# Spreading the first convolutions of later batches over seven ticks less in a chain of long convolutions and a Haar layer

## The chip, the cores and the metric

The kernel runs on one core of one Trainium2 chip. The metric is the device time of one execution in microseconds (us), as the median of several runs. TensorE does the matmuls, VectorE and ScalarE read its results out of PSUM and do the element-wise work, SyncE and ScalarE issue the DMAs.

## The reference, cut to what matters

The input x has 4 batches of 64 channels of 256 x 256 float32 values. Four layers follow each other:

```python
x = conv(x, L0); x = conv(x, L1)      # long separable convolutions, zero padded, per channel, plus x * bias
f1 = haar2d(x)                        # all levels, along both axes
for i in range(2):
    f4 = einsum('bchw,oc->bohw', f1 * v[i], conv_w[i])      # mixes the channels
    acc += sign(f4) * relu(abs(f4) - tau[i])                # soft threshold
x = haar2d(acc, inverse=True) + x
x = conv(x, L3)
```

A convolution of one channel is two Toeplitz contractions, one along each axis. The Haar layer needs all 64 channels of a batch before it can mix them, and the last convolution needs the mixed coefficients of all rows.

## The kernel before

**Stages of one batch.** The function `convolutions` takes each channel through both first layers and the forward Haar transform, `mixing` takes 64 groups of coefficients through the channel mix and the threshold, and `inverse` takes each channel back through the inverse Haar transform and through the last convolution. Two thirds of the last convolutions of batches 0 to 2 are done in `inverse`; a third (`put_off`) are stored and done beside the mixing of batch 3 by `convolution`.

**Ticks.** No stage issues its work directly. Each puts its steps into a list of events through `at(tick, place, run, unit)`, and at the end the list is sorted by tick, then by place, and run in that order. So the tick of a step decides which other steps stand beside it in the program. The engines take their instructions in order; the framework adds the waits and may move independent instructions past each other on a queue.

**Steps of a channel in `convolutions`.** With its tick t: load at t; `first` of layer 0 at t+1 (contraction into the PSUM tile pa by lines 167 and 168, copied to a by ScalarE on line 176); `second` of layer 0 at t+2 (contraction into py, line 189 adds the bias term on VectorE into y); the same for layer 1 at t+3 and t+4, where `pairs` also makes the first Haar level along the row (lines 230 and 231 into the buffer sd) and stores the result in keep (line 232, by ScalarE's DMA queue). After every fourth channel, `levels` makes the other Haar levels of four channels in place in sd: three steps in three ticks, 14 VectorE operations (lines 240 and 241), each working on half the elements of the last. `down` then makes the Haar levels along the other axis by one matmul for each channel (pz, line 263), ScalarE copies it (line 267), and SyncE stores it in coef. The last `down` comes 11 ticks after the last channel's tick at most. sd has room for eight channels, so a group's levels and the next group's pairs don't share memory.

**Steps of a group in `mixing`.** mix (four px matmuls, line 308; scaling by VectorE on line 325 and by eight ScalarE operations on line 327), shrink (Abs and Sign on ScalarE, lines 333 and 334; a subtraction on line 335), signed (line 340), add (line 344, into the large buffer z), one tick apart. The next group starts one tick later.

**Steps of a channel in `inverse`.** fetch (load r; copy a column of z into zc on ScalarE, line 361; before channel 0, `butterfly` on z), rows (pw, lines 368 and 369; copy and subtraction into w, lines 371 and 372), cols (pu, line 381; t on line 385, u on lines 388 and 389), then the two contractions of the last convolution and the store of its result.

**What sets the ticks around the change.** Mixing of batch b takes the ticks from `start` on. The inverse begins at `end`, which is `start` + 67, and the next mixing begins at `end` + 64 or three ticks after the next batch's coefficients are ready, whichever is later. The convolutions of batch b+1 have to lie somewhere beside these. `spread(begin, end)` gives the 64 channels evenly spaced ticks from begin to just below end:

```python
def spread(begin, end, n=C):
    return [begin + i * (end - begin - 1) // (n - 1) for i in range(n)]
```

`ahead` is 64 for batch 1 and three ticks before `start` for batches 2 and 3.

Of the kernel before, what the change touches and what calls it, by code (L numbers as in the profile page):

```python
# [37 lines left out]
def conv_seq_kernel(ctx, tc, x, fz, fw, bias, decay, haar, haar_row, factors, vt, taut, wmix, out):  # L38
# [116 lines left out]
    def toeplitz(layer, c, name):  # L155

        t = tp.tile([P, 2, S], F32, name=name, tag="toep")
        nc.sync.dma_start(t, ap(pads[layer], c * 2 * ROW, [[1, P], [ROW, 2], [1, S]]))
        return t

    def bank(name):
        return psm.tile([P, 2, S], F32, name=name, tag="mm")
# [7 lines left out]
    def first(b, st, key, layer, new):  # L170
        def run(c):
            s = st[c]
            ps = bank(f"p{new}_{b}_{c}")
            contract(ps, s[key], s[layer][:, 0, :])
            a = io.tile([P, 2, S], F32, name=f"{new}_{b}_{c}", tag="mid")
            nc.scalar.copy(a, ps)  # L176
            s[new] = a

        return run

    def second(b, st, key, layer, res, new, tag, ahead=None):
        def run(c):
            s = st[c]
            if ahead is not None:
                s[ahead] = toeplitz(ahead, c, f"t{ahead}_{b}_{c}")
            ps = bank(f"p{new}_{b}_{c}")
            contract(ps, s[key], s[layer][:, 1, :])
            y = io.tile([P, 2, S], F32, name=f"{new}_{b}_{c}", tag=tag, bufs=BUFS[tag])
            nc.vector.scalar_tensor_tensor(y, s[res], bsb[:, layer, c : c + 1], ps, ALU.mult, ALU.add)  # L189
            s[new] = y  # L190

        return run
# [12 lines left out]
    def at(tick, place, run, unit):  # L205
        events.append((tick, place, len(events), run, unit))

    def stream(stages, ticks):

        for unit, tick in enumerate(ticks):  # L210
            for s, stage in enumerate(stages):
                if stage is not None:
                    at(tick + s, -s, stage, unit)

    def convolutions(b, ticks, in_parts=False):

        st = {}

        def load(c):
            xt = io.tile([P, 2, S], F32, name=f"x_{b}_{c}", tag="in", bufs=4)  # L220
            nc.sync.dma_start(xt, x[b, c].rearrange("(k p) w -> p k w", p=P))
            st[c] = {"x": xt, 0: toeplitz(0, c, f"t0_{b}_{c}")}

        last_second = second(b, st, "a1", 1, "y0", "y1", "res")

        def pairs(c):
            last_second(c)
            v = st.pop(c)["y1"].rearrange("p k (w e) -> p k w e", e=2)
            t = sd[:, c % 8]
            nc.vector.tensor_add(t[:, :, 0, :], v[:, :, :, 0], v[:, :, :, 1])  # L230
            nc.vector.tensor_sub(t[:, :, 1, :], v[:, :, :, 0], v[:, :, :, 1])  # L231
            nc.scalar.dma_start(keep[b][c], t)

        def levels(steps):
            def run(n):
                t = sd[:, n % 2 * 4 : n % 2 * 4 + 4]
                for step in steps:
                    v = t[:, :, :, 0, :].rearrange("p c k (w e) -> p (c k) w e", e=2 * step)
                    even, odd = v[:, :, :, 0], v[:, :, :, step]
                    nc.vector.tensor_sub(odd, even, odd)  # L240
                    nc.vector.scalar_tensor_tensor(even, even, 2.0, odd, ALU.mult, ALU.subtract)

            return run

        parts = {}

        def split(c):

            w = parts[c] = mx.tile([P, 2, 2, S], F32R, name=f"sp_{b}_{c}", tag="f4")
            t = sd[:, c % 8].rearrange("p k e w -> p k (e w)")  # L250
            nc.scalar.copy(w[:, 0], t)
            nc.vector.tensor_tensor(w[:, 1], t, w[:, 0].bitcast(F32), ALU.subtract)

        def down(c):
            ps = bank(f"pz_{b}_{c}")
            flat = "p k w -> p (k w)"
            if in_parts:
                for i in range(2):
                    nc.tensor.matmul(
                        ps.rearrange(flat), hbr, parts[c][:, i].rearrange(flat), start=(i == 0), stop=(i == 1)  # L260
                    )
            else:
                nc.tensor.matmul(
                    ps.rearrange(flat), hbt, sd[:, c % 8].rearrange("p k e w -> p (k e w)"), start=True, stop=True
                )
            t = io.tile([P, 2, S], F32, name=f"co_{b}_{c}", tag="co", bufs=BUFS["co"])
            nc.scalar.copy(t, ps)
            nc.sync.dma_start(coef[b][:, c].rearrange("k p w -> p k w"), t)

        stream(  # L270
            [load, first(b, st, "x", 0, "a0"), second(b, st, "a0", 0, "x", "y0", "y", ahead=1), first(b, st, "y0", 1, "a1"), pairs],
            ticks,
        )
        for n in range(C // 4):
            end = ticks[4 * n + 3] + 4
            for s, steps in enumerate([(1,), (2, 4), (8, 16, 32, 64)]):
                at(end + 1 + s, 1, levels(steps), n)
            for j in range(4):
                if in_parts:
                    at(end + 3 + j, 2, split, 4 * n + j)  # L280
                at(end + 4 + j, 2, down, 4 * n + j)
        return ticks[-1] + 11
# [128 lines left out]
    def convolution(which, ticks):  # L411

        for (b, c), tick in zip(which, ticks):
            st = {}

            def load(c, b=b, st=st):
                u = io.tile([P, 2, S], F32, name=f"v_{b}_{c}", tag="in", bufs=4)
                nc.sync.dma_start(u, late[b, c])
                st[c] = {"u": u, 2: toeplitz(2, c, f"t2_{b}_{c}")}

            for s, stage in enumerate([load, *last(b, st)]):
                at(tick + s, -s, stage, c)


    def spread(begin, end, n=C):
        return [begin + i * (end - begin - 1) // (n - 1) for i in range(n)]
# [4 lines left out]
    ready = convolutions(0, range(C), in_parts=True)  # L431
    ahead = C
    start = ready + 3
    for b in range(B):
        mixing(b, start, 8 if b + 1 < B else 6)
        end = start + groups + 3
        if b + 1 < B:
            ready = convolutions(b + 1, spread(ahead, end + 2))
        else:
            convolution(  # L440
                [(i, c) for i in range(B - 1) for c in sorted(put_off)], spread(start - 2, end + 2, (B - 1) * len(put_off))
            )
        inverse(b, end, put_off if b + 1 < B else ())

        start = max(end + C, ready + 3)
        ahead = start - 3
# [112 lines left out]
```

## Time and profile before

The time is 3088.14 us as the median of three runs (3085.73 to 3089.94); the profiled execution spans 3090.0 us. The table cuts that execution at the first and the last px matmul of each mixing and at channel 20's row transform in the inverse. Busy times are in us.

| stretch | from, to (us) | length | PE | DVE | ACT | DMA share |
|---|---|---|---|---|---|---|
| mixing, batch 0 | 479.7 to 901.3 | 421.6 | 414.6 | 382.3 | 308.4 | 0.65 |
| mixing to inverse, batch 0 | 901.3 to 1005.8 | 104.5 | 98.1 | 75.2 | 57.7 | 0.71 |
| rest of the inverse, batch 0 | 1005.8 to 1142.4 | 136.6 | 136.6 | 110.2 | 86.8 | 0.78 |
| mixing, batch 1 | 1142.4 to 1601.4 | 459.0 | 452.6 | 403.5 | 317.1 | 0.67 |
| mixing to inverse, batch 1 | 1601.4 to 1712.1 | 110.7 | 106.1 | 78.7 | 60.4 | 0.71 |
| rest of the inverse, batch 1 | 1712.1 to 1848.6 | 136.5 | 136.5 | 110.1 | 86.7 | 0.78 |
| mixing, batch 2 | 1848.6 to 2309.4 | 460.8 | 454.1 | 403.4 | 317.0 | 0.67 |
| mixing to inverse, batch 2 | 2309.4 to 2419.7 | 110.3 | 104.8 | 78.4 | 60.2 | 0.73 |
| rest of the inverse, batch 2 | 2419.7 to 2552.3 | 132.6 | 132.6 | 109.4 | 86.2 | 0.79 |

PE is TensorE, DVE VectorE, ACT ScalarE. A row's idle TensorE time is its length less its PE time. A busy TensorE isn't TensorE at its peak, since a matmul's recorded end overlaps the next one's start; how far matmuls lie apart is read from their starts in the timeline.

### The profile page before, as it was taken

What the parts mean: (1) busy time and instruction counts of PE and PEld (TensorE: products, weight loads), DVE (VectorE), ACT (ScalarE), POOL (GpSimd) and SP (SyncE); (2) the same over time, 40 slices, a digit from 0 to 9 for tenths busy, and PEclk for the clock granted to TensorE, in tenths of its full rate; (3) what the DMA queues carried; (4) which work ended last, traced back from release to release, by engine and by line L of the source; (5) the groups of instructions that cost most, each with busy time, mean ns of one, the idle gap of its engine ahead of it and who ended that gap; (6) DMA issues with size and microseconds to landing.
All of it is one profiled execution on the core that took longest, in us unless ns stands there. A gap on an engine that the chain in (4) does not pass through costs nothing. (4 is left out here: it accounts for less than half of the span.)

```text
span 3090.0 us, 50474 instructions
## 1 busy us (share of the span) xinstructions
PE 3004.4 (97%) x16944; PEld 2615.3 (85%) x16944; DVE 2523.4 (82%) x4453; ACT 1926.9 (62%) x4054; POOL 0.2 (0%) x4
## 2 busy tenths in 40 slices
PE   5999999999999999999999999999999999999999
PEld 3999988888888888888887888888887888888998
DVE  6667677999987878888886879888886889998776
ACT  1333336777765656667665656666774667887554
POOL 0000000000000000000000000000000000000000
PEclk9999999999999999999999999999999999999999
DMA  4777877666667876666667776666667777877676
GB/s 118 217 230 230 234 227 211 196 193 197 195 193 228 238 223 196 195 207 199 194 205 216 236 229 196 199 195 204 198 195 218 235 238 228 236 233 212 210 211 188
DMA packets 555573, 649.26 MB, mean 210 GB/s; under 512 B 39761, under 2 KB 440500, under 8 KB 555188
## 3 DMA queue, kind: packets, MB, share of 16 engines
q1 hardware_dynamic: 439316, 493.18, 56.5%
q10 hardware_dynamic: 116000, 152.87, 13.7%
q8 instruction: 136, 2.23, 0.3%
q14 instruction: 121, 0.99, 0.1%
HBM read 426.40 MB, written 219.48 MB: 209 GB/s over the span
## 5 line engine op out<-in xcount | busy, mean ns | idle before, releaser
L167 PE MATMUL py<-t,a 128*128 128x256 f32 x3072 | 926.0, 383 | 27.9 <-ACT a L176 24.6
L176 ACT COPY a<-pa 128x512 f32<-128x512 f32 x768 | 458.7, 597 | 466.3 <-PE pa L168 330.7
L168 PEld LDWEIGHTS py<-t,a 128*128 128x128 f32 x3072 | 584.1, 190 | 79.4
L327 ACT ACTIVATE f<-px,vt 128x64 f32<-128x64 f32 x1920 | 422.0, 329 | 352.7 <-DVE f L325 348.3
L167 PEld LDWEIGHTS py<-t,a 128*128 128x128 f32 x3072 | 488.4, 191 | 126.1 <-issue 63.2
L168 PE MATMUL py<-t,a 128*128 128x128 f32 x3072 | 590.6, 274 | 0.0
L308 PE MATMUL px<-wb,f 128*128 128x256 f32 x2048 | 494.2, 380 | 4.3 <-ACT f L327 4.3
L308 PEld LDWEIGHTS px<-wb,f 128*128 128x128 f32 x2048 | 366.0, 191 | 44.1 <-ACT f L327 6.7
L335 DVE TENSOR_TENSOR mag<-mag,vt 128x1024 f32<-128x1024 f32 x256 | 312.2, 1219 | 36.0 <-ACT mag L333 34.8
L167 PE MATMUL pa<-t,x 128*128 128x256 f32 x1024 | 307.5, 382 | 9.4 <-DMA t<-pad 9.3
L340 DVE SCALAR_TENSOR_TENSOR mag<-mag,f 128x1024 f32<-128x1024 f32 x256 | 311.4, 1216 | 0.3
L167 PE MATMUL pa<-t,y 128*128 128x256 f32 x1024 | 306.3, 381 | 1.2 <-DVE y L189 0.9
L333 ACT ACTIVATE mag<-f 128x1024 f32<-128x1024 f32 x256 | 283.9, 1109 | 12.6 <-DVE z L344 6.8
L361 ACT COPY zc<-z 128x512 f32<-128x512 f32 x256 | 281.9, 1102 | 3.9 <-DVE z L199 2.6
L371 ACT CAST w<-pw 128x512 fp32r<-128x512 f32 x256 | 150.2, 587 | 212.3 <-PE pw L369 201.3
L334 ACT ACTIVATE f<-f 128x1024 f32<-128x1024 f32 x256 | 272.0, 1062 | 9.7 <-DVE sd L231 2.4
L189 DVE SCALAR_TENSOR_TENSOR y<-y,bsb,py 128x512 f32<-128x512 f32 x256 | 190.1, 743 | 104.5 <-PE py L168 103.7
L385 DVE SCALAR_TENSOR_TENSOR t<-r,pu 128x512 f32<-128x512 f32 x256 | 175.3, 685 | 86.6 <-PE pu L381 79.6
L189 DVE SCALAR_TENSOR_TENSOR y<-x,bsb,py 128x512 f32<-128x512 f32 x256 | 190.1, 743 | 62.6 <-PE py L168 54.0
L167 PE MATMUL pa<-t,u 128*128 128x256 f32 x772 | 234.1, 385 | 1.1 <-DVE y L189 0.7
L189 DVE SCALAR_TENSOR_TENSOR y<-u,bsb,py 128x512 f32<-128x512 f32 x193 | 143.8, 745 | 102.4 <-PE py L168 98.7
L168 PEld LDWEIGHTS pa<-t,x 128*128 128x128 f32 x1024 | 195.7, 191 | 26.9
(65 smaller groups left out, 4370.7 us busy)
## 6 DMA issues: line engine op xcount, KB each, us to landing
t<-pad SPq DMA_DIRECT2D x768, 256.0 KB, 3.9
x<-in_x SPq DMA_DIRECT2D x256, 256.0 KB, 3.9
keep<-sd ACTq DMA_DIRECT2D x256, 256.0 KB, 3.3
coef<-co SPq DMA_DIRECT2D x256, 256.0 KB, 3.1
f<-coef SPq DMA_DIRECT2D x256, 256.0 KB, 3.9
r<-keep SPq DMA_DIRECT2D x256, 256.0 KB, 3.4
out_y<-y ACTq DMA_DIRECT2D x256, 256.0 KB, 3.6
late<-u ACTq DMA_DIRECT2D x63, 256.0 KB, 2.6
```

Source lines behind the costliest of these rows:

```text
L167: nc.tensor.matmul(ps[:, m, :], src[:, 0, m * P : (m + 1) * P], t[:, ::-1], start=True, stop=False)
L168: nc.tensor.matmul(ps[:, m, P:], src[:, 1, m * P : (m + 1) * P], t[:, : P - 1 : -1], start=False, stop=True)
L176: nc.scalar.copy(a, ps)
L189: nc.vector.scalar_tensor_tensor(y, s[res], bsb[:, layer, c : c + 1], ps, ALU.mult, ALU.add)
L308: nc.tensor.matmul(ps[:, h, q, :], f[:, q, h * P : (h + 1) * P], wb.rearrange("p r n -> p (r n)"), start=True, stop=True,)
L327: nc.scalar.mul(f4[:, j], px[:, j], scale(g, 0)[:, j : j + 1])
L333: nc.scalar.activation(mag, f4, AF.Abs)
L334: nc.scalar.activation(f4, f4, AF.Sign)
L335: nc.vector.tensor_sub(mag, mag, over(g, 1, 16))
L340: nc.vector.scalar_tensor_tensor(mag, mag, 0.0, st[g]["f4"], ALU.max, ALU.mult)
L361: nc.scalar.copy(a, z[:, :, :, c].rearrange("p h (i k) -> p h k i", k=2))
L385: nc.vector.scalar_tensor_tensor(t, st[c]["r"], 0.5, ps, ALU.mult, ALU.add)
```

## The change

It moves the end of the spread of the convolutions of batches 1 to 3 from two ticks after the inverse's first tick to five ticks before it. It is meant to bring the Haar levels of the last channels into mixing ticks, so that they don't stand between the inverse's operations on VectorE.

```diff
         end = start + groups + 3
         if b + 1 < B:
-            ready = convolutions(b + 1, spread(ahead, end + 2))
+            ready = convolutions(b + 1, spread(ahead, end - 5))
         else:
```

Loads of batch 1 then lie in ticks 64 to 138 in place of 64 to 145, those of batch 2 in ticks 205 to 269 in place of 205 to 276, those of batch 3 in 336 to 400 in place of 336 to 407. The inverse stages begin at ticks 144, 275 and 406 both ways.

## The prediction

> **What bounds the kernel now.** I read the page from the top: busy shares, slices, then the waits of TensorE stage by stage, then the timeline at the longest of them.
>
> ```profile
> span 3090.0 us, 50474 instructions
> PE 3004.4 (97%) x16944; PEld 2615.3 (85%) x16944; DVE 2523.4 (82%) x4453; ACT 1926.9 (62%) x4054; POOL 0.2 (0%) x4
> PEclk9999999999999999999999999999999999999999
> ```
>
> TensorE is the bound and its clock is full. The change removes no work, so only idle TensorE time can move. Busy time hides part of that, so I took start-to-start distances from the timeline: a pair of 128x256 f32 matmuls takes 0.43 us, 128x128 0.22, 128x512 0.86, a px group 1.73, one contraction 1.31. Summed over the program this is 2955 us; what is longer is lost: 122 us, of which 22 at the start. By stage (times from the trace; small excesses included):
> - mixing of batches 0, 1, 2: lost 14.5, 11.0, 12.8 us, sum 38.3;
> - transition, from the last px to channel 20 of the inverse: 9.7, 8.9, 8.6, sum 27.2;
> - the rest of an inverse: 3.9 each, no single wait above 0.25.
>
> The waits of TensorE in the mixing of batch 2 (1848.6 to 2309.4), then in the transition of batch 1 (1601.4 to 1712.1); columns: total, times, longest.
>
> ```profile
> PE py L167 <- ACT a L176: 6.1, 9, 1.0
> PE pa L167 <- DVE t L385: 0.3, 1, 0.3
> ...
> PE pz L263 <- DVE sd L241: 3.4, 1, 3.4
> PE pu L381 <- DVE w L372: 0.5, 1, 0.5
> ```
>
> The two stages wait for different things: mixing for ScalarE's copy of the first contraction, the transition for the Haar levels. The timeline shows why. First a mixing tick of batch 2's convolutions without a full set of contractions, then the end of a level chain in batch 1's inverse:
>
> ```profile
> 1394.49 0.60 PE L308 MATMUL px<-wb,f 128*128 128x256 f32 x2
> 1395.13 0.63 ACT L176 COPY a<-pa 128x512 f32<-128x512 f32 x1
> 1395.81 0.70 PE L167 MATMUL py<-t,a 128*128 128x256 f32 x2 [0.72 <-ACT a L176]
> ...
> 1660.87 0.69 DVE L240 TENSOR_TENSOR sd<-sd 128x512 f32<-128x512 f32 x1 [1.63 <-DMA coef<-co]
> ...
> 1673.86 0.18 DVE L241 SCALAR_TENSOR_TENSOR sd<-sd 128x8 f32<-128x8 f32 x1
> 1674.18 1.89 PE L263 MATMUL pz<-sd,hbt 128*128 128x512 f32 x2 [3.44 <-DVE sd L241]
> ```
>
> The levels ran from 1660.9 to 1674.0, 13 us for 14 operations, because VectorE takes its queue in order and inverse work stood between them. The 1.89 us matmul pair (normally 1.02) ran at half clock:
>
> ```profile
> 1674.10:1677.90 3.80, 3.72 (x11) 2.59 (x11) 0.00 (x0) 1.04 (x2) 0.00 (x0) 0.55 0.23 77
> ```
>
> [...] a 3.4 us wait, then a granted 0.55 over 3.8 us, 1.7 us lost; waits of 2.4 us in the other transitions cost no clock.
>
> **The change part by part.** Ticks follow from the code. Mixing of batch b runs start to start+63, the inverse from end = start+67; starts are 77, 208, 339, 470 with and without the change, since the inverse sets them.
>
> *Mixing of batches 1 and 2.* 64 loads over 72 ticks become 64 over 65: before, every eighth tick gets none; after, one channel a tick except at the end. A tick without its full set is where the 1.0 us waits sit: at channels 16, 24, 32, 40, 47/48 and 56, the first contraction and its second stand only two px matmuls apart, and ScalarE is still busy with scaling, Abs and Sign. Single waits there lost 7.9 and 8.4 us; I leave 1.5 and 0.9 (those at the start of the stage, which stay). Gain 6.4 + 7.5. Work per tick rises from 7.1 to 7.7 us on TensorE and from 6.3 to 6.6 on VectorE (mixing 3.5 by start distance, a convolution 3.1): VectorE gets more slack, not less.
>
> *Mixing of batch 0.* 64 over 82 ticks become 64 over 75. Some 17 short ticks lost 8.8 us, 0.5 each; some 10 remain, between 0.5 and the 0.86 of batches 1 and 2, so about 7. Gain 2. Small excesses that go with the short ticks: gain 1. Mixing in all: 17.
>
> *Transitions: what is removed.* Convolutions no longer run into inverse ticks, so the 13 us level chains of groups 13 and 14 go into mixing ticks, where a chain does not hold TensorE (no level wait in the mixing rows above).
>
> *Transitions: what is added.* The same convolutions were TensorE's work while mixing drained into the inverse. Before, five ticks after the last px held 6 us each of them; after, between the last px and the first row transform stand only two contractions and five pz, 6.9 us. I followed the chain in the changed program's own queue order for batch 1, in us from the end of px 62, with durations of the rows above it in the profile:
> - px 63 ends 6.5. ScalarE: scaling to 9.7, copy of the last a 10.2, Abs 11.3, Sign 12.8. VectorE: threshold 12.5, pairs' first operation 13.1, signed 14.3, pairs 14.9, add 15.6. TensorE waits 0.7 for the a.
> - ScalarE then has pz copies, which wait for the coefficient store two copies earlier (issued 11.9, landing 3.1 later, so 15.2), and the keep store, before the first zc: 15.9 to 17.0. TensorE is out of work at 14.4: wait 2.5. Second zc and w copies: waits 0.8 and 0.7.
> - Group 15's levels may start when the keep store has landed: 15.8 + 3.7 (the trace: issued 1657.20, first level 1660.87) = 19.5. In VectorE's queue w 0, w 1, t 0 and u 0 stand between them: 26.7. pz of channel 60, behind pu 0, waits from 21.2 to 26.8: 5.6, with pw 2 and all later TensorE work queued behind it.
>
> Sum 0.7 + 2.5 + 0.8 + 0.7 + 5.6 = 10.3, with semaphore steps 11.5. The 5.6 us is longer than the 3.4 that halved the clock above: 1.7 or a little less on average. Small excesses 1. About 14 a transition against 9.1, so 3 x 4.9 = 15 lost. Nothing else is queued there that could hide it: inverse work all hangs on z. The three transitions have nearly the same queue order (batch 0 has its pz of channel 55 earlier).
>
> *Unchanged:* start-up, the rest of the inverses, the last batch with its deferred convolutions, the traffic (coefficients of a batch are read 50 ticks after they are written, before and after).
>
> Sum: -17 + 15 = -2 on 3088.1; I say 3087. The costs that no row shows are the new transition wait: lower bound 8 (the keep store and levels hidden, only the drain of about 5 and the w steps), upper 18 (another store wait of 3[...]).
>
> **The rivals.**
> 1. *The drain is hidden and the gain stands.* The level chain without inverse work between its operations is 4.6 us (start distances 1.2 + 1.7 + 1.7), and ScalarE might run ahead. Transitions stay at 9: -17 + 0 gives 3071. For it: TensorE's idle hurts only while the chain is longer than 6.9 us of work. Against: the add needs 9 us after px 63 by the durations alone.
> 2. *The drain costs more than the gain.* 17 a transition (stores late, clock halved each time) gives 3 x 8 = +24, mixing gains 14: 3098, slower. For it: TensorE has some 1 us of work a tick over six ticks. Against: the last batch's transition, with 2.6 us of deferred convolutions a tick, lost only 5.4 us.
>
> **How the numbers follow.** Gain and loss cancel: 0.45, 3087. Rival 1: 0.31. Rival 2: 0.24. 0.2% is 6.2 us, so faster is below 3082 and slower above 3094; the three cases fall one on each side, and give the chances. The range takes in rival 1 except for a mixing gain above 17 with a short drain, and rival 2 as computed: 3073 to 3099.
>
> **What would show it.** Right: waits of py on a in the mixing of batches 1 and 2 fall from 6 us to about 1, in batch 0's they stay at 5 to 7; in each transition one wait of pz on sd of 5 to 6 us, a wait of pw on zc of 2 to 3, a clock below 1 in one or two of them; starts of the next mixing 1142.4, 1848.6, 2552.3 move by under 8 us. Wrong: transitions with no wait above 3 us (rival 1), or VectorE waits in full mixing ticks, or a transition of more than 16 us lost (rival 2).

## The result, and the profile after

The changed kernel takes 3099.66 us (3097.55 to 3101.34, four runs), the kernel before 3086.93 us beside it (3083.40 to 3089.94, four runs): a ratio of 1.0041, with an interval of 1.0024 to 1.0059. It is some 13 us slower. The forecast was 3087, in a range of 3073 to 3099; its second rival, 3098, came closest.

The page of the kernel after, the same lines as before:

```profile
span 3099.5 us, 50401 instructions
...
PE 3005.9 (97%) x16944; PEld 2620.1 (85%) x16944; DVE 2531.8 (82%) x4453; ACT 1924.2 (62%) x4054; POOL 0.2 (0%) x4
```

The number of matmuls is the same, and their recorded busy time is 1.5 us longer. Nothing on these lines shows where 13 us went. So I used the measure of the prediction again: how much longer two successive matmuls on TensorE stand apart than such a pair needs. Both kernels are cut at the last px matmul of group 62 (a group earlier than in the prediction, so that the drain of mixing lies in one stage only).

| us lost on TensorE | before | after | moved | forecast |
|---|---|---|---|---|
| start-up | 25.8 | 23.8 | -2.0 | 0 |
| mixing, batches 0, 1, 2 | 13.8, 11.0, 12.7 | 11.6, 7.8, 7.1 | -11.0 | -17 |
| transition, batches 0, 1, 2 | 10.4, 8.9, 8.6 | 15.9, 17.7, 17.0 | +22.7 | +15 |
| all the rest | 30.8 | 30.4 | -0.4 | 0 |
| whole program | 122.0 | 131.3 | +9.3 | -2 |

The 9.3 us is, to within 0.2 us, the difference of the two profiled executions (3090.0 and 3099.5); the medians differ by 12.7. Both large terms went the way that the prediction said, and both were mis-sized: 6 us too much gain, 8 us too little loss. How the miss divides depends on the cut. At the prediction's own cut, the last px matmul, mixing moved by about -7 us (38.3 to 31) and the transitions by about +19 (27.2 to 46, which is 15 to 16 us each), since 1 to 2 us a batch, lost just before that matmul, then count as mixing.

The waits of TensorE in the transition of batch 1 (1635 to 1719 us); columns: total, times, longest:

```profile
PE pz L263 <- DVE sd L241: 5.5, 1, 5.5
PE pw L368 <- ACT zc L361: 3.3, 2, 2.2
PE py L167 <- ACT a L176: 2.3, 2, 1.6
```

This is the list that the prediction drew up: one long wait of pz for levels, two waits of the row transform for the column of z, a wait for the copy a. Before, this stretch had one wait of 3.4 us and a few short ones. The timeline of the kernel after shows the steps in order of time:

```profile
1648.07 0.69 DVE L344 TENSOR_TENSOR z<-mag 128x512 f32<-128x512 f32 x1
...
1648.19 0.33 ACTq L232 DMA_DIRECT2D keep<-sd  x1
1648.79 1.05 ACT L361 COPY zc<-z 128x512 f32<-128x512 f32 x1 [0.89 <-DVE z L344]
...
1649.89 0.49 PE L368 MATMUL pw<-hrow,zc 128*128 128x128 f32 x2 [2.21 <-ACT zc L361]
...
1651.89 0.79 PE L368 MATMUL pw<-hrow,zc 128*128 128x128 f32 x2 [1.07 <-ACT zc L361]
1652.05 0.69 DVE L240 TENSOR_TENSOR sd<-sd 128x512 f32<-128x512 f32 x1 [3.29 <-DMA coef<-co]
...
1659.58 0.17 DVE L241 SCALAR_TENSOR_TENSOR sd<-sd 128x8 f32<-128x8 f32 x1
...
1659.90 2.04 PE L263 MATMUL pz<-sd,hbt 128*128 128x512 f32 x2 [5.50 <-DVE sd L241]
```

The last add to z ends at 1648.76; until then no row transform can start, and TensorE has run out of convolutions. The last keep store goes out at 1648.19, and the first level of the last group starts 3.86 us later, which fits the 3.7 us from keep store to level that the prediction took from before. (The releaser shown there, a coef store, is inferred; the store that the levels need is keep.) The levels end at 1659.75. Then pz starts, and behind it on TensorE's queue the row transform of the third column (1661.74), whose zc had been copied by 1653.34.

Two columns in this excerpt tell more. The row transform at 1649.89 takes 0.49 us and the same one at 1651.89 takes 0.79: the granted clock was 0.50 already **before** the 5.5 us wait. Here it is in batch 1, in stretches of 3.41 us, as long as the half clock lasted in the kernel before. The columns are the length, the busy time (and count) of TensorE, its weight loads, VectorE, ScalarE and GpSimd, then the clock, the DMA share and GB/s:

```profile
1645.03:1648.45 3.42, 2.65 (x7) 0.87 (x5) 3.42 (x6) 2.01 (x3) 0.00 (x0) 1.00 0.67 164
1648.45:1651.86 3.41, 0.93 (x6) 0.69 (x6) 0.31 (x1) 2.61 (x4) 0.00 (x0) 1.00 0.76 263
1651.86:1655.27 3.41, 2.50 (x8) 1.79 (x8) 2.97 (x5) 3.05 (x4) 0.00 (x0) 0.50 0.22 72
1655.27:1658.69 3.42, 0.00 (x0) 0.00 (x0) 3.28 (x11) 0.00 (x0) 0.00 (x0) 0.50 0.29 77
1658.69:1662.10 3.41, 2.20 (x4) 1.20 (x5) 0.93 (x5) 0.12 (x1) 0.00 (x0) 0.50 0.02 5
1662.10:1665.51 3.41, 3.41 (x13) 3.00 (x12) 1.40 (x3) 2.02 (x3) 0.00 (x0) 0.50 0.23 77
```

In the trace the half clock lasts 13.65 us in batches 1 and 2 and 10.24 us in batch 0. Between its start-up and its end the kernel before had one such stretch, of 3.41 us.

In the mixing of batch 1 (1143.9 to 1630 us) the waits for a became fewer, and no shorter. Before there were 8 of them, 5.5 us together, the longest 1.0 (1142.4 to 1594 us); after:

```profile
PE py L167 <- ACT a L176: 3.6, 4, 1.2
```

Over the three mixings after, the same row has 6.8, 3.6 and 1.7 us, in 9, 4 and 3 waits: 12.1 us.

### The profile page after: what moved, and what is told of

Its sections match the earlier page's. It is cut to its first block, busy times and chain, and to the rows that moved or that the text cites. A ratio compares the mean times of both kernels' runs of the same rounds, so it can differ in the third digit from the quotient of the medians.

```text
span 3099.5 us, 50401 instructions
## 1 busy us (share of the span) xinstructions
PE 3005.9 (97%) x16944; PEld 2620.1 (85%) x16944; DVE 2531.8 (82%) x4453; ACT 1924.2 (62%) x4054; POOL 0.2 (0%) x4
## 4 chain that ended last, share of the span: by engine, by line
PE 48%; DVE 11%; ACT 5%; DMA 4%; issue 2%; ACTq 0%; DVEq 0%; SPq 0%
PE pa L167 10%; PE py L167 10%; PE px L308 6%; PE py L168 5%; PE pa L168 5%; PE pu L381 4%; PE pw L368 4%; ACT f L327 2%; DVE mag L340 2%; DMA keep<-sd 2%; PE pz L263 2%; PE pw L369 2%; DVE mag L335 2%; DVE sd L240 1%; DVE sd L241 1%
## 5 line engine op out<-in xcount | busy, mean ns | idle before, releaser
L333 ACT ACTIVATE mag<-f 128x1024 f32<-128x1024 f32 x256 | 284.8, 1112 | 11.6 <-DVE z L344 6.8
L240 DVE TENSOR_TENSOR sd<-sd 128x512 f32<-128x512 f32 (+6 forms) x448 | 164.7, 368 | 70.5 <-DMA keep<-sd 26.8
```

Source lines behind the costliest of these rows:

```text
L333: nc.scalar.activation(mag, f4, AF.Abs)
```

## The experiments

Thirteen kernels ran. The losses come from the profiled executions; a time is a median, and its ratio is to the kernel before on the same chip. A profiled execution may lie some us off its kernel's median (e4's span was 3087.6, e11's 3073.5), so stages are compared by their losses and kernels by their ratios. No losses are given for e2, whose unused matmuls would count as work.

| kernel | time, us | ratio to before | mixing lost | transitions lost |
|---|---|---|---|---|
| before | | 1 | 37.5 | 27.9 |
| after | 3099.66 | 1.0041 [1.0024, 1.0059] | 26.5 | 50.6 |
| e1 after, late down | 3086.47 | 0.9999 [0.9990, 1.0007] | 23.8 | 37.5 |
| e2 after, unused matmuls | 3095.27 | 1.0021 [1.0011, 1.0030] | | |
| e3 spread shifted | 3092.88 | 1.0015 [1.0008, 1.0021] | 34.4 | 21.2 |
| e4 spread to end - 2 | 3081.74 | 0.9979 [0.9972, 0.9986] | 38.7 | 26.7 |
| e5 end - 2, late down | 3080.26 | 0.9968 [0.9960, 0.9977] | 37.2 | 20.9 |
| e6 after, late levels and down | 3087.78 | 0.9998 [0.9989, 1.0006] | 30.2 | 37.5 |
| e7 after, keep store on SyncE | 3107.73 | 1.0050 [1.0033, 1.0067] | 29.6 | 53.2 |
| e8 before, late down | 3081.99 | 0.9977 [0.9970, 0.9984] | 36.8 | 20.1 |
| e9 after, scaling late | 3104.42 | 1.0063 [1.0047, 1.0080] | 30.8 | 47.9 |
| e10 before, scaling late | 3079.17 | 0.9975 [0.9968, 0.9982] | 26.9 | 26.1 |
| e11 e5, scaling late | 3078.45 | 0.9974 [0.9965, 0.9983] | 29.4 | 22.5 |
| e12 after, no levels in mixing | 3082.53 | 0.9980 [0.9971, 0.9989] | 8.5 | 49.8 |
| e13 after, scaling late, keep on SyncE | 3105.96 | 1.0055 [1.0040, 1.0070] | 28.6 | 55.0 |

Two questions were open: what makes the transitions lose 23 us, and why mixing gained 11 us and not 17.

### The transitions

**e1: the last group's pz out of the row transforms' way.** In the transition pz of channel 60 waits for levels with all row transforms queued behind it. Here the last group's `down` comes six ticks later, when its levels are long done.

```diff
-                at(end + 4 + j, 2, down, 4 * n + j)
+                at(end + 4 + j + (6 if n == C // 4 - 1 and not in_parts else 0), 2, down, 4 * n + j)
```

> The changed kernel, with the four pz matmuls of each later batch's last group put six ticks later, so that none of them stands in TensorE's queue ahead of the inverse's row and column transforms while the group's levels run. Theory A (in each transition TensorE waits 5.9 us for those levels, and loses more at half clock because of it): the waits of pz on sd in the transitions go, each transition falls from about 17 us lost to 8 to 10, and the time from 3100 to 3073 to 3080 us. Rival B (the drain of the mixing chain through z and zc is what binds, and the wait on the levels only stands where another would): the wait moves to pw or pu, and the time stays at 3094 to 3100 us.

3086.47 us, 13 us less than after, and the transitions lost 13.1 us less. The waits of TensorE in batch 1's transition (1620 to 1710 us):

```profile
PE pw L368 <- ACT zc L361: 3.1, 2, 2.2
PE py L167 <- ACT a L176: 2.5, 2, 1.8
PE pa L167 <- issue: 1.8, 1, 1.8
```

The row of pz is gone, and with it part of the half clock: the mean granted clock of the profiled execution is 0.997, of after's 0.994. The waits for zc and a are the same as after: these are the drain, and they remain. So the result lies between the two expectations: the queue position of pz explains 13 of the 22.7 us, and the remaining 37.5 us is still 10 more than before.

**e6: the levels moved as well.** In e1 a new wait of 1.8 us before a first contraction of the inverse was left, and the last group's levels were a suspect for it. Here they too come later (levels by five ticks, `down` by six).

```diff
-                at(end + 1 + s, 1, levels(steps), n)
+                at(end + 1 + s + (5 if n == C // 4 - 1 and not in_parts else 0), 1, levels(steps), n)
```

> The changed kernel with the last group's levels five ticks later and its pz six ticks later, so that neither stands among the first operations of the inverse. With the pz alone later the time was 3086 us and a wait of 1.8 us of pa 0 on u 0 was left, behind levels on VectorE. Theory A with filler (what then remains is the drain: 1.8 + 0.8 us on a, 2.4 + 1.1 on zc, in each transition, and no clock): that wait goes, 2 to 4 us a transition, 3076 to 3082 us. Rival B (levels that come later meet more inverse work and hold it up as in the kernel before): 3086 us or more.

3087.78 us, the same as e1, and the wait is still there:

```profile
PE pa L167 <- issue: 1.6, 1, 1.6
```

The edit moved less than its ticks say. In the finished order the first two level operations, the largest, still stand ahead of u of channel 0, which this contraction reads; only the smaller ones come behind it:

```profile
1650.30 0.69 DVE L240 TENSOR_TENSOR sd<-sd 128x512 f32<-128x512 f32 x1 [3.47 <-DMA coef<-co]
1651.51 0.69 DVE L241 SCALAR_TENSOR_TENSOR sd<-sd 128x512 f32<-128x512 f32 x1
...
1655.21 0.42 DVE L389 TENSOR_TENSOR u<-t 128x256 f32<-128x256 f32 x1
...
1655.73 0.67 PE L167 MATMUL pa<-t,u 128*128 128x256 f32 x2 [1.65 <-issue]
```

So moving the smaller levels gained nothing, and whether this wait comes from the two large ones or belongs to the drain, with the waits for a and zc, is not shown.

**e2: the clock.** After, with unused matmuls of 0.43 us in each transition, 5 before the first row transform, 2 before the second and 12 before pz of channel 60, to keep TensorE busy while it would wait.

```diff
+            if b + 1 < B and c < 2:
+                warm(b, 5 if c == 0 else 2)
...
+            if c == C - 4 and not in_parts:
+                warm(b, 12)
```

> The changed kernel, with 5, 2 and 12 additional matmuls of 0.43 us in each of the three transitions, ahead of pw 0, pw 1 and pz 60, where TensorE waited 2.4, 1.2 and 5.9 us. Their results are not used. They keep TensorE busy and its clock up, and don't shorten the chain. Theory A (the half clock of 10 to 14 us in each transition costs 2.1, 3.8 and 3.8 us): the granted clock stays at 1, and the time falls by about 9 us, to 3091 us. Rival C (the clock costs nothing, since TensorE waits anyway): 3100 us; and if the additional matmuls push the chain back, above 3100 us.

3095.27 us, and the granted clock is 1.00 in all three transitions. The gain over after is 4 us by the medians, 6 by the ratios (1.0041 and 1.0021, whose intervals overlap) and 7 by the profiled executions (3099.5 and 3092.4). What is left of the long wait in the trace (1630 to 1715 us):

```profile
PE pz L270 <- DVE sd L246: 0.5, 1, 0.5
```

The extra matmuls fill the waits and don't shorten the chain on VectorE; the gain is what the half clock had added. It is less than the 9 us expected, and about what the prediction allowed (three times 1.7, so 5 us) or a little more. This kernel's lines from the edits on are a few further down: L270 is L263 of the others, L246 is L241.

**e3: the same rate as before, but everything seven ticks later.** This keeps convolutions in the inverse ticks and delays their start.

```diff
-            ready = convolutions(b + 1, spread(ahead, end - 5))
+            ready = convolutions(b + 1, spread(ahead + 7, end + 2))
```

> One channel a tick as in the changed kernel, but seven ticks later: spread(ahead + 7, end + 2), so the last channels end where those of the kernel before end. Theory A (full ticks gain in mixing, and the lost filler at the end costs): the transitions lose 9 us each or less, the waits of py on a in the mixing of batches 1 and 2 stay at 3 to 4 us as in the changed kernel, but the first seven mixing ticks have no convolutions, where VectorE's 3.5 us a tick bind against 1.7 us of TensorE: 12 us each in batches 1 and 2, so 3095 to 3105 us. Rival D (the levels' place, in mixing or in the inverse, sets the time, and filler doesn't matter): as the kernel before or faster, 3075 to 3087 us.

The transitions lost 21.2 us, less than before, and the mixing 34.4. What the two stages gained was lost again where ticks now lack work: the stretch ahead of the first mixing lost 34.2 us in place of 25.8, and the first eight groups of the mixings of batches 1 and 2 some 5 us each in place of 2. That is less than the 12 us each that was expected, and the time, 3092.88, stayed below the range of theory A. The profiled execution (3090.1) was no longer than that of before, so the 4 us between the medians are not traced to a stage. Still, a stretch without convolutions cost in each place where it was put; after puts it into the drain, e3 ahead of the mixing and at its start.

**e4: half the dose.** The spread ends at `end - 2`.

```diff
-            ready = convolutions(b + 1, spread(ahead, end - 5))
+            ready = convolutions(b + 1, spread(ahead, end - 2))
```

> The spread ends at end - 2 in place of end - 5 or end + 2, so three of the seven ticks are given back to the transition. Theory A: the loss in the transitions lies between 9 and 17 us each, about 12, mixing waits lie between, and the time is 3087 to 3095 us. Rival D (place of the levels): a step, as the changed kernel (3100) if the last levels are ahead of the inverse's first row, as the kernel before (3087) if not.

3081.74 us, faster than before by 0.2% and below what either theory said. With end + 2, end - 2 and end - 5 the ratios are 1, 0.9979 and 1.0041: the gain comes with the first ticks taken away, and the loss with the last three. In which stage the gain lies is not shown: the profiled execution was the slowest of e4's twenty, and its two stages lost as much as those of before. Batch 1's transition here (1612 to 1705 us) has the long row at half its length:

```profile
PE pz L263 <- DVE sd L241: 2.7, 1, 2.7
PE py L167 <- ACT a L176: 0.9, 1, 0.9
PE pw L368 <- ACT co L267: 0.8, 1, 0.8
```

**e5 and e8: late down with end - 2, and with before.** The edit of e1 on e4 and on the kernel before.

> The spread that ends at end - 2, with the four pz matmuls of the last group six ticks later. With end - 2 alone the transitions lost 9.6, 9.6 and 7.5 us, of which one wait of pz on sd of 2.7 us and the half clock after it are about 5 each. Theory A: those go, so 10 to 15 us below end - 2 alone: 3068 to 3073 us (ratio 0.994). Rival B (the wait moves to the next operation that needs VectorE, as it partly did when the same was done to the changed kernel): 3077 to 3082 us.

> The kernel before with the four pz of the last group of each later batch six ticks later. There one wait of pz on sd of 1.9 to 3.4 us, once with half clock, stands in each transition. Theory A: each goes with what follows it, 2 to 5 us, so 3075 to 3081 us (ratio 0.996 to 0.998). Rival B (the wait moves): 3086 to 3089 us.

e5 took 3080.26 us, where rival B had it; its ratio, 0.9968, is the lowest here. e8 took 3081.99, a ratio in theory A's range, with 20.1 us lost in the transitions in place of 27.9. So pz standing in the queue costs some 8 us in the kernel before as well (7 by the ratio). The edit is worth 13 us in after, 7 in before, and 1.5 (by the medians) to 3.4 us (by the ratios) with end - 2, where the intervals touch.

### The mixing

In after, every wait of TensorE for a in the mixing of batch 1 falls on a channel that is 3 more than a multiple of four: 23, 31, 39 and 51. These ticks have their full set of contractions, so the prediction's reason (ticks without one) can't hold for them. The timeline of the first, all of VectorE's and ScalarE's part that matters:

```profile
1305.70 1.89 PE L308 MATMUL px<-wb,f 128*128 128x256 f32 x8
...
1310.38 0.68 DVE L325 TENSOR_TENSOR f<-px,vt 128x512 f32<-128x512 f32 x1
...
1311.10 1.75 ACT L327 ACTIVATE f<-px,vt 128x64 f32<-128x64 f32 x8 [2.58 <-DVE f L325]
...
1312.69 0.63 ACT L176 COPY a<-pa 128x512 f32<-128x512 f32 x1
...
1313.37 0.70 PE L167 MATMUL py<-t,a 128*128 128x256 f32 x2 [0.99 <-ACT a L176]
```

The a that TensorE waits for stands behind eight scalings (its contraction pa had ended at 1308.90 us), these wait 2.58 us for VectorE's half of the same scaling, and that comes 4.7 us after the first px matmul. Three causes can be told apart: ScalarE held at the keep store (e7), ScalarE's order of scaling and copy (e9 to e11), VectorE itself (e12).

**e7: the keep store on SyncE's queue,** so that ScalarE isn't held until the pairs are done.

```diff
-            nc.scalar.dma_start(keep[b][c], t)
+            nc.sync.dma_start(keep[b][c], t)
```

> The changed kernel with the keep store issued by SyncE in place of ScalarE. ScalarE's queue then doesn't stop at a store that waits for the pairs on VectorE. Theory E (in full mixing ticks TensorE's remaining waits for a come from ScalarE standing at the keep store, behind levels on VectorE; this is where the expected mixing gain fell short by 6 us): waits of py on a fall from 22 to under 12 us in all, and the time by 6 to 10 us, to 3090 to 3094 us. Rival F (ScalarE's own work, scaling, Abs and Sign, sets the waits): they stay, 3097 to 3102 us[...].

3107.73 us; the mixing lost 29.6 us and the transitions 53.2. The ratio doesn't differ from that of after beyond the intervals, and nothing is gained: the store alone doesn't hold a.

**e9, e10, e11: the scaling behind the copy a.** ScalarE's half of the scaling becomes a step of its own at place 0.5 of the tick, with `mix` at -1; in the finished order three scalings, the copy a and five scalings follow each other in most ticks.

```diff
-            for j in range(n, 16):
-                nc.scalar.mul(f4[:, j], px[:, j], scale(g, 0)[:, j : j + 1])
...
+        def scaled(g):
+            f4, px = st[g]["f4"], st[g]["px"]
+            for j in range(16 - n_act, 16):
+                nc.scalar.mul(f4[:, j], px[:, j], scale(g, 0)[:, j : j + 1])
...
+            at(start + g, 0.5, scaled, g)
```

> The kernel after, with ScalarE's half of the scaling put behind the copy of the first contraction of the same tick, so that on ScalarE's queue three scalings, the copy a, and five scalings follow each other, where eight scalings stood ahead of a. Theory G: the shortfall in the mixing gain is copies a that stand behind eight scalings (1.75 us), which themselves start late because they wait for VectorE's half; a comes 1.1 us earlier, the waits of py on a in the three mixings (8, 4 and 3 of them, 11.6 us together) fall to about 3 us, the mixing loss from 26.5 to 18, and the time is 3090 to 3094 us. Theory H: the work of a tick on ScalarE and VectorE as a whole sets when a is there, and its order only decides who waits: the waits move to other operations, the mixing loss stays at 26 and the time at 3099 to 3101. The transitions stay at 50 us under both.

> The kernel before with the same edit of the queue order. Theory G: the mixing loss of before (37.5 us) falls by 8 to 14 without any change of the spread, since its waits of py on a have the same cause and the ticks without a full set only make it likelier; transitions stay at 28, the time is 3074 to 3080 us. Theory H: no change, 3086 to 3089. If the ticks without a full set are what matters, as the prediction had it, the waits of before fall by less than those of after.

> The spread to end - 2, the last group's down six ticks later, and the same edit of the queue order: the gains should add if they are of different stages. Without the last edit it took 3080.3 us with 37.2 us lost in the three mixings and 20.9 in the transitions. Theory G: mixing loss 26 to 29, time 3069 to 3073. Theory H: 3079 to 3082.

The answer differs by kernel. In before the edit took 10.6 us from the mixing loss, and the time fell to 3079.17, ratio 0.9975: there theory G was right. In after it took nothing: 30.8 us lost, 3104.42 us. The waits became shorter, none over 0.7, and more, 21 in place of 16 over the three mixings; their sum, 11.6 us, was nearly that of after (12.1). In before they fell from some 18 to 11.5 us. If the ticks without a full set were what mattered, before should have gained less than after; it gained more, which speaks against the prediction's reason in before too. In e11 the profiled execution lost 7.8 us less in the mixing than e5, but the medians of e11 and e5 don't differ beyond their intervals, so no gain is shown there. One tick of e9 suggests why an edit that helps before doesn't help after:

```profile
1494.81 1.22 DVE L339 TENSOR_TENSOR mag<-mag,vt 128x1024 f32<-128x1024 f32 x1
1495.30 0.58 ACT L176 COPY a<-pa 128x512 f32<-128x512 f32 x1 [2.92 <-DVE sd L231]
...
1498.46 0.52 ACT L332 ACTIVATE f<-px,vt 128x64 f32<-128x64 f32 x2 [2.58 <-DVE f L325]
1498.87 0.58 ACT L176 COPY a<-pa 128x512 f32<-128x512 f32 x1
```

ScalarE stands idle twice in this tick, 2.92 us for the pairs (ahead of the keep store) and 2.58 us for the scaling, and both times VectorE releases it. VectorE had just run levels.

**e12: no levels in the mixing.** After without the level operations of the first 14 groups of batches 1 to 3. This leaves out that part of the forward Haar transform; all else stays, the last two groups' levels too.

```diff
-                at(end + 1 + s, 1, levels(steps), n)
+                if in_parts or n >= C // 4 - 2:
+                    at(end + 1 + s, 1, levels(steps), n)
```

> The kernel after without the Haar levels (14 VectorE operations for each group of four channels) of the first 14 groups of batches 1 to 3; this leaves out that part of the forward Haar transform. The last two groups keep theirs, so the transitions are as in after. Theory V: in full ticks VectorE's stretch of level operations (4.4 us at a time) delays its half of the scaling and the pairs; ScalarE, whose queue holds its own half of the scaling and the keep store ahead of the copies a, stands with it, and TensorE waits for a. Without the levels the waits of py on a in the three mixings fall from 11.6 us to under 2, the mixing loss from 26.5 to 13 to 17, and the time to 3086 to 3091 us. Theory S: ScalarE's own order and work set the wait (eight scalings ahead of a): then the waits stay above 8 and the time is 3096 to 3101.

The mixing lost 2.4, 2.2 and 3.9 us in place of 11.6, 7.8 and 7.1, the transitions the same as after (49.8), and the time was 3082.53, 17 us less than after: both fell further than theory V had said. Of all waits for a in the three mixings one of 0.4 us was left. The tick that corresponds to the one of after above:

```profile
1304.24 1.89 PE L309 MATMUL px<-wb,f 128*128 128x256 f32 x8
...
1306.24 0.68 DVE L326 TENSOR_TENSOR f<-px,vt 128x512 f32<-128x512 f32 x1
...
1306.96 1.75 ACT L328 ACTIVATE f<-px,vt 128x64 f32<-128x64 f32 x8 [2.59 <-DVE f L326]
1308.56 0.64 ACT L176 COPY a<-pa 128x512 f32<-128x512 f32 x1
...
1310.76 0.60 PE L167 MATMUL py<-t,a 128*128 128x256 f32 x2
```

VectorE's scaling now starts 2.0 us after the first px matmul (4.7 after), ScalarE's scaling 2.7 (5.4 after), and the copy a starts 2.7 us sooner in the tick, 2.2 us before its contraction, which stands without a wait. ScalarE still idles 2.59 us at the scaling, as in every tick, and nothing is lost by it. ScalarE has the same work in the same order in both kernels. So what makes a late in after are the levels on VectorE. A view of the levels of one group in after shows how late (VectorE's timeline):

```profile
1299.88 0.68 DVE L325 TENSOR_TENSOR f<-px,vt 128x512 f32<-128x512 f32 x1
1302.23 0.69 DVE L240 TENSOR_TENSOR sd<-sd 128x512 f32<-128x512 f32 x1 [1.67 <-DMA x<-in_x]
...
1306.48 0.39 DVE L241 SCALAR_TENSOR_TENSOR sd<-sd 128x128 f32<-128x128 f32 x1
...
1310.38 0.68 DVE L325 TENSOR_TENSOR f<-px,vt 128x512 f32<-128x512 f32 x1
```

From one scaling to the next pass 10.5 us, while px groups come every 7.8 us on average. Between them are six level operations and a wait of 1.7 us ahead of the first. That wait is for a DMA; twelve such waits, 9.9 us together, stand ahead of levels in this stage, and the profile puts nine of them down to the keep store. Over the whole stage VectorE was busy for 418.56 of 486.10 us, so the average hides this. e12 takes away the stretch of operations, the waits ahead of it and the load on VectorE (355.86 of 481.40 us are left) all at once. Which of these three counts is not shown: no kernel ran with the same levels spread evenly over the ticks.

**e13: both queue positions at once.** After with the edits of e7 and e9.

> The kernel after with ScalarE's half of the scaling behind the copy a and the keep store on SyncE's queue, both at once: each alone left the mixing loss at 29 to 31 us. Theory V: VectorE's lateness reaches ScalarE through both, so that only both together let a run ahead; three scalings still stand ahead of a, so the waits of py on a fall to 3 to 6 us from 11.6, the mixing loss to 18 to 22, and the time is 3095 to 3103 us (the store on SyncE alone cost 8 us elsewhere). If the waits stay at 10 or more, VectorE's lateness reaches the copies in another way, or it isn't VectorE.

3105.96 us, mixing loss 28.6, where 18 to 22 was expected. The waits for a were still 11.2 us in sum (3.6, 3.9, 3.7). So VectorE's lateness can't be passed by with these two edits; three scalings still stand ahead of a, and that the rest of the way goes through them is only argued.

## Why the prediction was wrong

**What bounds it.** Right: TensorE's matmuls didn't change, and what moved is idle or half-clock TensorE time. In the profiled executions the two stages named lost 11.7 us more, and all the rest 2.4 us less, most of it (2.0) in the start-up, which the prediction had as unchanged.

**Mixing, forecast -17, measured -11.0.** Batch 0 was right (2 to 3 forecast, 2.2 measured). Batches 1 and 2 gained 3.2 and 5.6 us in place of 6.4 and 7.5 and their small excesses. The step that failed: "a tick without its full set is where the 1.0 us waits sit", and, from mean work per tick, "VectorE gets more slack, not less". Slack as a mean was true (7.7 us of TensorE work to 6.6 of VectorE's), but a group's levels come in a stretch, and two scalings around it lie 10.5 us apart. The prediction also said that a level chain in mixing ticks doesn't hold TensorE since no level wait stands in its rows. e12 shows that it does, under another name: TensorE waits for a, ScalarE for VectorE's scaling. In after these levels cost 18.0 us of the 26.5 lost in mixing. The change was meant to bring the level chains of the last groups into just these ticks; what those add is not shown, since e12 keeps the last two.

**Transitions, forecast +15, measured +22.7.** The chain was right, and four of the five waits of the prediction's ledger were there near their size: in batch 1 it had 5.6 us for pz on the levels (5.9 by start distances), 2.5 for the first row transform (2.4), 0.8 for the second (1.2), 0.7 for the a of the last pairs (0.8). The fifth, 0.7 for the copies into w, shows in no row of that transition. The terms of the sum that were mis-sized:
- the half clock, put at 1.7 or less in each, as for the 3.41 us of half clock in before: it lasted 10.24, 13.65 and 13.65 us and cost 2.1, 3.8 and 3.8 us by the start distances, 9.7 in all, of which e2 won back 4 to 7;
- a wait for the copy a in the last channel's first layer, missing from the ledger: 1.1, 1.8 and 1.3 us. It stands just ahead of the last px matmul, so the prediction's own cut counts it as mixing.

Together these are 8.8 us more than the ledger had for the three (9.7 less 5.1, and 4.2), close to the 8.6 by which 15.9, 17.7 and 17.0 exceed 14 each. By the prediction's own cut the transitions come near their 14, at 15 to 16, and most of the miss lies in mixing. The bound "upper 18", the author's estimate, held in all three. The prediction gave this case a chance of 0.24 and its number, but the forecast took the clock as "a little less than 1.7".

**The argument against the second rival** was that the last batch's transition, with 2.6 us of deferred convolutions a tick, lost only 5.4. It does have work there, and that is what after lacks; it spoke for the rival.

**Not forecast:** a spread that ends three ticks later (e4) is faster than both kernels. Some ticks less were worth having, and seven were too many.

## What to carry to other kernels

Work that looks like an obstacle at the boundary of two stages may be the filler that covers the pipeline's drain: before moving it, count how much work of the bottleneck engine is left between the last input of one stage and the first result of the next, and what stands at the head of its queue there. A mean of busy time per tick can hide that an engine gets its work in stretches (here 10.5 us from one scaling to the next, with a px group every 7.8 us); look at the distance between two of the operations that others wait for. When a wait names one engine, follow the releaser's own wait one step back before concluding whose work is too slow.

## What the runs showed of the hardware

In the transition of batch 1 of the kernel before, a wait of 3.44 us was followed by half clock, a granted 0.55 over 3.80 us. Between start-up and end the clock stood at 0.50 once in that kernel, for 3.41 us, and three times in the kernel after, for 10.24, 13.65 and 13.65 us.

In batch 1 of the kernel after the granted clock was 1.00 in the 3.41 us from 1648.45 us, in which the waits of 2.21 and 1.07 us had left 0.93 us of matmuls (recorded busy time, whose ends are modelled). It was 0.50 in the next stretch, ahead of the 5.5 us wait, still 0.50 in the one from 1662.10 us, which was busy throughout, and 1.00 in the 3.41 us after that. In batch 0 of the kernel before a wait of 2.4 us, longer than either of these two, cost no clock: the granted clock of that transition (901.3 to 1005.8 us) was 1.00. So in these traces the length of the single wait doesn't tell by itself whether it costs clock. (The prediction has 2.4 us for both other transitions of before; in batch 2 the longest was 1.9.)

The unused matmuls of e2 shortened no chain, kept the granted clock at 1.00 and were worth 4 to 7 us.
